# A four-layer graph megakernel: layer transitions in groups of five node blocks, narrower waits of tiles, node results in PSUM, and one edge list's bounds moved

## The chip, the cores and the metric

The kernel runs on one core of a Trainium2 chip. Its engines are PE (TensorE, matmul and transposes), DVE (VectorE), ACT (ScalarE), POOL (GpSimd, which here issues the indirect gathers and scatters) and SP (which issues the plain DMAs); each works through a queue of its own. The metric is the device time of one execution in microseconds, the median of several runs; lower is better.

## The reference

A node array x of 3125 rows by 256 floats goes through four pairs of layers. Each layer adds its result to x, and each sees the normalised rows of x.

```python
x = x + gat(norm(x), edges_A)                    # gnn0: 8 heads, relu
x = x + layernorm(z + top2_moe(z)), z = norm(x)  # ffn0: 16 experts, 2 per row
x = x + gat(norm(x), edges_A)                    # gnn1: 8 heads
x = x + layernorm(z + moe(z)), z = norm(x)       # ffn1: 2 of 8 experts for all rows
x = x + gat(gat(norm(x)))                        # gnn2: g2a (8 heads), g2b (1 head)
x = x + moe(z), z = norm(x)                      # ffn2: 4 experts, scores from attention over edges_B
x = x + edge_attention(norm(x), edge_attr)       # gnn3
x = x + moe(norm(x))                             # ffn3: 8 experts, two hidden layers, batch norm
```

`norm` subtracts a row's mean and divides by its standard deviation. `gat` is attention over a list of edges: a projection h of every node, a logit per edge from the source's and the target's h, a softmax over the edges that arrive at one node, and the weighted sum of the sources' h. List A has 50,000 edges, sorted by target; list B has 65,536 in random order.

## The kernel before

Nodes lie in 25 blocks of 128 (`NT` = 25, `NP` = 3200 with padding), one row per partition; `self.xs` holds x in SBUF for the whole run. Edges lie 128 partitions deep: A with 391 per partition, B with 512. A scheduler (the tile framework) sets the order on each engine, from the program's order and the dependences between tiles; only the inner loops over edges are put on DVE and ACT by hand (`manual_schedule`). Memory comes in pools. A tile of a pool takes over bytes that an earlier tile used, and waits until that one's users are done.

A graph layer (`gat_once`) goes like this. `norm` computes `bn_stats` and `bn_aggr` of all 25 blocks (`stats`), one square root on ACT and one reciprocal, then 25 times z. `transposed` turns each z block into zT by PE with a copy by ACT. A projection per block follows (`hps`): its values and source logits go to a DRAM table by SP, its target logits into `D`, copied by DVE. `spread` scatters D (25 indirect DMAs of POOL, the `A_Z` scatter) to the first edge of each node, reads that back, and spreads it along the edges. Then comes the loop over edges: POOL gathers the sources' rows (`hg`, one indirect DMA for 128 edges), DVE and ACT weigh and accumulate them, and SP writes groups of eight columns back to `OUT`. `join_chunks` repairs the nodes whose edges cross partitions. `node_results` then gathers each node's row from OUT (`ng`, 25 gathers, in groups of `NB` = 5 blocks), divides by the sum of the weights, and hands the group to `use`, which adds it to x or writes it to z. For g2a, g2b and ffn2 the node's own term is added (`own`, in a tile `nown`). Both work in place in `ng`, and `ng` has three buffers.

For each list the kernel needs bounds, the first and last edge of every node (`bounds`): a comparison of 128 by 3200 and its sum on DVE, an index, then 25 gathers of whole rows of targets by POOL (`brow`), each counted by one DVE operation (`bjunk`), and some twenty small ones. `marks` computes where runs of edges begin, and penalties (`penG`) for the scans. List B has to be sorted first; that runs on DVE beside gnn0's gathers (`sort_packed`), and B's bounds and marks are the end of the same function. They are first needed in ffn2.

The expert layers: ffn0 takes logits of all blocks (`token_logits`), top 2, and scatters rows to 40 slots of one expert each; at the end POOL gathers two results per row (`y`), and `add_layernorm` (L1044 to L1046 and the addition to x, L762) normalises and adds. ffn1 picks two experts for everybody from the mean of zT, and runs each over seven blocks of up to 512 rows. ffn2 deals its 28 units of expert work (4 experts by 7 blocks of rows) to the eight groups of 64 gathers of list B, six to each group until none is left; in each group the copy of a part of the edge features from DRAM to DRAM (`copy_features`) follows the group's units in the program, and SP issues it in that order. ffn3 runs softmax, loads batch-norm columns, adds the biases (`gb`), and then 8 experts by 7 blocks.

Of the kernel before, what the change touches and what calls it, by code (L numbers as in the profile page):

```python
# [9 lines left out]
F32 = mybir.dt.float32  # L10
# [4 lines left out]
ALU = mybir.AluOpType  # L15
AX = mybir.AxisListType
PSUM = bass.MemoryType.PSUM
DRAM = bass.MemoryType.DRAM

P = 128  # L20
# [13 lines left out]

class Edges:
# [3 lines left out]
class Kernel:  # L39
    def __init__(self, tc, ctx, a, out):  # L40
        self.tc, self.nc, self.a, self.out = tc, tc.nc, a, out
        nc = self.nc
        self.const = ctx.enter_context(tc.tile_pool(name="const", bufs=1))
        self.dram = ctx.enter_context(tc.tile_pool(name="dram", bufs=1, space=DRAM))
# [39 lines left out]
    def columns(self, pool, aps, rows_each, name):  # L84
# [5 lines left out]
        with tc.tile_pool(name=name + "_l", bufs=1) as lp, tc.tile_pool(name=name + "_p", bufs=1, space=PSUM) as pp:  # L90
# [9 lines left out]
    def stats(self, pool, src, nt, name):  # L100

        nc = self.nc
        mv = pool.tile([P, nt, 2], F32, name=name + "_mv")
        for t in range(nt):
            st = pool.tile([P, 6], F32, name=name + "_st", bufs=4)
            nc.vector.bn_stats(st, src[:, t, :])  # L106
            nc.vector.bn_aggr(mv[:, t, :], st)
        rs = pool.tile([P, nt], F32, name=name + "_rs")
        nc.scalar.activation(rs, mv[:, :, 1], AF.Sqrt, bias=self.eps5)  # L109
        nc.vector.reciprocal(rs, rs)  # L110
        return mv, rs

    def norm(self, pool, z):

        mv, rs = self.stats(pool, self.xs, NT, "ln")
        for t in range(NT):
            self.nc.vector.tensor_scalar(z[:, t, :], self.xs[:, t, :], mv[:, t, 0:1], rs[:, t : t + 1], op0=ALU.subtract, op1=ALU.mult)  # L117

    def transposed(self, psum, z, zT):

        nc = self.nc
        for t in range(NT):
# [3 lines left out]
            nc.scalar.copy(zT[:, :, t * P : (t + 1) * P], ps)  # L126

# [14 lines left out]
    def edges_by_destination(self, name, src_ap, dst_ap, E, zc):  # L142
# [10 lines left out]
        with tc.tile_pool(name="s0", bufs=1) as sp:  # L153
# [21 lines left out]
            with tc.tile_pool(name="sp0", bufs=1, space=PSUM) as pp:  # L175
# [25 lines left out]
    def counting_sort(self, L, src, dst, dstf):  # L201
# [4 lines left out]
        with tc.tile_pool(name="s1", bufs=1) as sp, tc.tile_pool(name="s2", bufs=2) as wp:  # L206
# [21 lines left out]
            with tc.tile_pool(name="sp1", bufs=1, space=PSUM) as pp:  # L228
# [21 lines left out]
            with tc.tile_pool(name="sp2", bufs=2, space=PSUM) as pp:  # L250
# [98 lines left out]
    def sort_packed(self, name, src_ap, dst_ap, E, zc):  # L349
# [7 lines left out]
        with ExitStack() as scope:  # L357
# [17 lines left out]
            table = self.dram.tile([P, T], F32, name=name + "_dst")  # L375
            nc.sync.dma_start(out=table, in_=dstf)
            self.bounds(L, sp, table, dstf)
            dnext = sp.tile([P, 1], F32, name="dnext")
            nc.vector.memset(dnext, -5.0)
            nc.sync.dma_start(out=dnext[: P - 1, :], in_=table[1:, 0:1])  # L380
            self.marks(L, sp, dstf, dnext)
        return L

    def bounds(self, L, sp, table, dstf):
# [4 lines left out]
        with tc.tile_pool(name="bw", bufs=3) as wp, tc.tile_pool(name="bp", bufs=1, space=PSUM) as pp:  # L389
# [78 lines left out]
    def chain_marks(self, L, sp, dstf):  # L468
# [14 lines left out]
        with tc.tile_pool(name="cmp", bufs=1, space=PSUM) as pp:  # L483
# [34 lines left out]
    def spread(self, L, D, z, n, tag):  # L518
# [6 lines left out]
        with tc.tile_pool(name=tag + "z", bufs=1) as sp:  # L525
# [12 lines left out]
    def att_weights(self, pool, load_w, a_src, a_dst, H, dh, tag):  # L538
# [5 lines left out]
        with tc.tile_pool(name=tag + "aw", bufs=2) as sp:  # L544
# [9 lines left out]
    def gat_once(self, L, tag, load_z, load_w, a_src, a_dst, H, dh, eps, loops, use):  # L554
# [11 lines left out]
        with tc.tile_pool(name=tag + "k", bufs=1) as kp:  # L566
# [9 lines left out]
            with tc.tile_pool(name=tag + "t", bufs=1) as sp, tc.tile_pool(name=tag + "tp", bufs=3, space=PSUM) as pp:  # L576
# [3 lines left out]
                self.transposed(pp, z, zT)  # L580
                for t in range(NT):
# [7 lines left out]

            R = kp.tile([P, W], F32, name="R")  # L590
            mR = kp.tile([P, H], F32, name="mR")
            with tc.tile_pool(name=tag + "e", bufs=1) as sp, tc.tile_pool(name=tag + "v", bufs=4) as vp, \
                    tc.tile_pool(name=tag + "vp", bufs=2, space=PSUM) as pp, \
# [79 lines left out]
    def node_results(self, L, tag, OUT, H, dh, eps, own, use):  # L673
# [6 lines left out]
        with tc.tile_pool(name=tag + "n", bufs=3) as np_:  # L680
            for t in range(0, NT, NB):
# [4 lines left out]
                r = np_.tile([P, NB, H], F32, name="nr")  # L686
                den = gv[:, :, :, dh]
                val = gv[:, :, :, :dh]
                wide = lambda x: x.unsqueeze(3).to_broadcast([P, NB, H, dh])
                if own is not None:  # L690

                    mx = np_.tile([P, NB, H], F32, name="nmx")
# [9 lines left out]
                    nc.vector.tensor_tensor(c, c, r.unsqueeze(1).to_broadcast([P, 2, NB, H]), ALU.mult)  # L702
                    ho = np_.tile([P, NB, Fh], F32, name="nown")
                    nc.vector.tensor_tensor(vals(ho), vals(own[1][:, t : t + NB, :W])[:, :, :, :dh], wide(c[:, 1]), ALU.mult)
                    nc.vector.tensor_tensor(val, val, wide(c[:, 0]), ALU.mult)
                    nc.vector.tensor_tensor(val, val, vals(ho), ALU.add)
                else:
                    nc.vector.tensor_scalar(r, den, eps, None, op0=ALU.add)
                    nc.vector.reciprocal(r, r)
                    nc.vector.tensor_tensor(val, val, wide(r), ALU.mult)  # L710
                use(t, NB, val, np_)

    def join_chunks(self, L, tag, OUT, R, mR, H, dh):
# [5 lines left out]
        with tc.tile_pool(name=tag + "j", bufs=1) as sp, tc.tile_pool(name=tag + "jp", bufs=1, space=PSUM) as pp:  # L719
# [44 lines left out]
    def normed(self, pool):  # L764
        z = pool.tile([P, NT, C], F32, name="z")
        self.norm(pool, z)
        return z
# [7 lines left out]
    def gnn0(self, L):  # L775
        nc, tc, a = self.nc, self.tc, self.a
        with tc.tile_pool(name="g0", bufs=1) as sp:
# [771 lines left out]
```

## Time and profile before

| | |
|---|---|
| time, median of 3 runs | 6270.55 us (6269.11 to 6270.8) |
| the profiled execution | 6277.97 us, its span 6275.9 us |
| granted TensorE clock, mean | 0.677 |
| busy | PE 41%, DVE 56%, ACT 13%, POOL 51% of the span |
| POOL `hg` of gnn0 and gnn1, 782 gathers | 969 ns each |
| POOL `hg` of ffn2, 512 gathers | 1014 ns each, 232.9 us idle before them |
| the edge loops: gnn0, gnn1, g2a, g2b, ffn2 | 152 to 655, 1440 to 1930, 2325 to 2814, 2941 to 3429, 3575 to 4327 us |
| the edge loop of gnn3 | 4556 to 5540 us |
| experts: ffn0, ffn1, ffn3 | 898 to 1272, 2066 to 2230, 5715 to 6275 us |

Times within the profile are microseconds from the start of the span, and durations are those of single instructions in it. A line names the engine, the source line, the operation and its tiles (output, arrow, inputs); in square brackets stands how long the engine had been idle, and what ended that. L129 is the helper that issues every gather, so gathers are told apart by their tiles. A row of the waits has the total in us, the number of times and the longest. PEclk is the granted clock of TensorE, in tenths of full speed. Between the stretches of the table lie the transitions from one layer to the next.

### The profile page before, as it was taken

What the parts mean: (1) busy time and instruction counts of PE and PEld (TensorE: products, weight loads), DVE (VectorE), ACT (ScalarE), POOL (GpSimd) and SP (SyncE); (2) the same over time, 40 slices, a digit from 0 to 9 for tenths busy, and PEclk for the clock granted to TensorE, in tenths of its full rate; (3) what the DMA queues carried; (4) which work ended last, traced back from release to release, by engine and by line L of the source; (5) the groups of instructions that cost most, each with busy time, mean ns of one, the idle gap of its engine ahead of it and who ended that gap; (6) DMA issues with size and microseconds to landing.
All of it is one profiled execution on the core that took longest, in us unless ns stands there. A gap on an engine that the chain in (4) does not pass through costs nothing. (4 is left out here: it accounts for less than half of the span.)

```text
span 6275.9 us, 39477 instructions
## 1 busy us (share of the span) xinstructions
PE 2584.4 (41%) x9265; PEld 1734.2 (28%) x9265; DVE 3504.1 (56%) x8011; ACT 794.9 (13%) x1810; POOL 3231.9 (51%) x3326
## 2 busy tenths in 40 slices
PE   2000049920001940002000499400566666639999
PEld 1000037710000530001000355200244555525555
DVE  6998611156886268884777411112778888871111
ACT  1000012210001110001000122100011111102222
POOL 3777430037774137775776576675077777730000
PEclk9555569955555975555555699755777666657999
DMA  5566335416663026663666234522377888730000
GB/s 193 191 225 221 124 115 169 156 57 197 223 219 109 14 64 224 220 218 109 212 212 204 52 109 123 154 55 67 144 256 262 264 268 262 264 123 16 10 11 26
DMA packets 398594, 963.74 MB, mean 154 GB/s; under 512 B 92478, under 2 KB 241053, under 8 KB 365966
## 3 DMA queue, kind: packets, MB, share of 16 engines
q1 hardware_dynamic: 236254, 538.71, 23.9%
q0 software_dynamic: 162096, 422.40, 23.2%
q8 instruction: 77, 1.26, 0.1%
q14 instruction: 167, 1.37, 0.1%
HBM read 611.38 MB, written 400.71 MB: 161 GB/s over the span
## 5 line engine op out<-in xcount | busy, mean ns | idle before, releaser
L724 PE MATMUL mRT<-ident,mR 128*8 128x128 f32 (+2 forms) x6 | 2.2, 372 | 2230.5 <-DVE mR L613 1356.0
L129 POOL DMA_INDIRECT hg<-g_H,A_tab x782 | 758.1, 969 | 240.4 <-issue 225.0
L668 DVE SCALAR_TENSOR_TENSOR hg<-hg,A_keep,v 128x264 f32<-128x264 f32 (+1 forms) x1368 | 666.2, 487 | 44.2
L129 POOL DMA_INDIRECT hg<-f_H,B_tab x512 | 519.3, 1014 | 232.9 <-issue 148.2
L724 PEld LDWEIGHTS mRT<-ident,mR 128*8 128x8 f32 (+2 forms) x6 | 0.5, 82 | 2233.1 <-issue 2233.1
L913 PE MATMUL ape<-we,aT 128*128 128x256 f32 x1564 | 493.6, 487 | 150.9 <-DVE kv L932 147.3
L129 POOL DMA_INDIRECT kv<-g_KV,A_tab x391 | 370.9, 949 | 295.3 <-issue 279.3
L660 DVE TENSOR_TENSOR v<-hg,e 128x1056 f32<-128x1056 f32 (+1 forms) x392 | 488.0, 1245 | 3.6 <-ACT e L652 3.6
L913 PEld LDWEIGHTS ape<-we,aT 128*128 128x128 f32 x1564 | 384.3, 252 | 251.1 <-DVE kv L932 164.4
L129 POOL DMA_INDIRECT hg<-g2a_H,A_tab x391 | 372.8, 953 | 119.2 <-issue 106.7
L129 POOL DMA_INDIRECT hg<-g2b_H,A_tab x391 | 371.5, 950 | 119.2 <-issue 114.0
L129 POOL DMA_INDIRECT q<-g_Q,A_tab x391 | 370.8, 948 | 120.1 <-issue 105.2
L1386 DVE TENSOR_TENSOR l<-hg,ad 128x256 f32<-128x256 f32 x8 | 6.3, 790 | 632.0 <-DMA hg<-f_H,B_tab 632.0
L1501 DVE SCALAR_TENSOR_TENSOR xs<-ps,g,xs 128x256 f32<-128x256 f32 x200 | 94.2, 484 | 458.1 <-PE ps L1500 458.1
L652 ACT ACTIVATE e<-d 128x72 f32<-128x72 f32 (+1 forms) x245 | 54.8, 223 | 2141.0 <-DVE d L649 2141.0
L125 PE MATMUL tr<-ident,z 128*128 128x128 f32 x450 | 109.5, 374 | 498.2 <-DVE z L117 434.6
L134 POOL DMA_INDIRECT A_Z<-D,A_first x100 | 99.3, 993 | 356.1 <-PE hps L584 223.4
L907 PE MATMUL apt<-ident,at 128*128 128x128 f32 x782 | 193.1, 382 | 196.6 <-ACT aT L909 188.2
L129 POOL DMA_INDIRECT y<-f_Y,pos x50 | 47.5, 949 | 398.3 <-DMA f_Y<-y 383.4
L125 PEld LDWEIGHTS tr<-ident,z 128*128 128x128 f32 x450 | 71.6, 200 | 535.1 <-ACT ln_rs L109 316.6
L1494 ACT ACTIVATE hT<-ps,bn 128x512 f32<-128x512 f32 (+1 forms) x224 | 162.4, 731 | 390.5 <-PE ps L1492 390.5
L930 DVE TENSOR_TENSOR kj<-kv,ape 128x512 f32<-128x512 f32 x196 | 135.9, 693 | 132.3 <-PE ape L913 112.1
(476 smaller groups left out, 6471.9 us busy)
## 6 DMA issues: line engine op xcount, KB each, us to landing
g_OUT<-hg SPq DMA_DIRECT2D x96, 1088.0 KB, 5.0
g2a_OUT<-hg SPq DMA_DIRECT2D x48, 1088.0 KB, 4.9
g_OUT<-kv SPq DMA_DIRECT2D x48, 1088.0 KB, 6.4
g2b_OUT<-hg SPq DMA_DIRECT2D x48, 1032.0 KB, 4.6
at<-attr SPq DMA_DIRECT2D x48, 1024.0 KB, 4.9
w<-in_L_ffn_w_dram SPq DMA_DIRECT2D x80, 512.0 KB, 3.9
attr<-in_edge_attr_dram SPq DMA_DIRECT2D x5, 6256.0 KB, 25.7
attr<-in_edge_attr_dram SPq DMA_DIRECT2D x3, 6240.0 KB, 26.9
```

Source lines behind the costliest of these rows:

```text
L125: nc.tensor.transpose(ps[:, k, :], z[:, t, k * P : (k + 1) * P], self.ident)
L129: return self.nc.gpsimd.indirect_dma_start(out=out, out_offset=None, in_=table, in_offset=bass.IndirectOffsetOnAxis(ap=idx, axis=0))
L134: i = self.nc.gpsimd.indirect_dma_start(out=table, out_offset=bass.IndirectOffsetOnAxis(ap=idx, axis=0), in_=in_, in_offset=None)
L652: nc.scalar.activation(e, d, AF.Exp)
L660: nc.vector.tensor_tensor(vals(v)[:, :k], vals(g[:, j0 : j0 + k, :W]), e[:, :, j0 + 1 : j0 + k + 1].rearrange("p h n -> p n h").unsqueeze( ...
L668: nc.vector.scalar_tensor_tensor(to, prev, L.keep[:, t + j0 + j : t + j0 + j + 1], v[:, j, :], op0=ALU.mult, op1=ALU.add)
L907: nc.tensor.transpose(pt[:, i2, k, :], at[t][:, j + i2, k * P : (k + 1) * P], self.ident)
L913: nc.tensor.matmul(pe[:, i2, :], aT[:, i2, k, :], we[:, k, :], start=(k == 0), stop=(k == KC - 1))
L930: nc.vector.tensor_tensor(kj[:, :k2], g[:, j : j + k2, :C], pe[:, :k2], ALU.add)
L1386: nc.vector.tensor_tensor(ln, g[:, :, W:].rearrange("p n h -> p h n"), ad[:, t : t + GB, :H].rearrange("p n h -> p h n"), ALU.add)
L1494: nc.scalar.activation(hT[:, f, :n], ps[:, :n], AF.Relu, bias=bn[l][1][:, c0 : c0 + 1], scale=bn[l][0][:, c0 : c0 + 1])
L1501: nc.vector.scalar_tensor_tensor(self.xs[:, t, :], po, g[:, t, e : e + 1], self.xs[:, t, :], op0=ALU.mult, op1=ALU.add)
```

## The change

It has seven parts.

1. All pools are opened with `reuse_waits="tile"`: a tile then waits for the users of the bytes that it takes over, and not for those of the whole pool before it.
2. `norm` and `add_layernorm` work in groups of five blocks: statistics, square root, reciprocal and z of one group, then the next.
3. `transposed` takes a function that is called after each block, so projections and logits follow each block's transposes in the program. `token_logits` adds its bias per group of five.
4. `node_results` puts the factors (`nf`) and the result (`nout`) into PSUM; `use` gets the result there. The tile `nown` is gone.
5. B's bounds and marks move out of `sort_packed` into `finish_sorted`, which is called after ffn1 and loads the sorted targets back from DRAM.
6. One tile z serves gnn0 to gnn2 with ffn0 and ffn1, instead of one for each layer.
7. ffn2's units of expert work are dealt by four to a group of gathers.

```diff
+def pool_of(tc, **kw):
+    return tc.tile_pool(reuse_waits="tile", **kw)
...
     def norm(self, pool, z):
-        mv, rs = self.stats(pool, self.xs, NT, "ln")
-        for t in range(NT):
-            self.nc.vector.tensor_scalar(z[:, t, :], self.xs[:, t, :], mv[:, t, 0:1], rs[:, t : t + 1], op0=ALU.subtract, op1=ALU.mult)
+        for t0 in range(0, NT, NB):
+            mv, rs = self.stats(pool, self.xs, t0, NB, "ln")
+            for t in range(NB):
+                self.nc.vector.tensor_scalar(
+                    z[:, t0 + t, :], self.xs[:, t0 + t, :], mv[:, t, 0:1], rs[:, t : t + 1], op0=ALU.subtract, op1=ALU.mult)
-    def transposed(self, psum, z, zT):
+    def transposed(self, psum, z, zT, then=None):
...
             nc.scalar.copy(zT[:, :, t * P : (t + 1) * P], ps)
+            if then is not None:
+                then(t)
...
-            self.bounds(L, sp, table, dstf)
-            dnext = sp.tile([P, 1], F32, name="dnext")
-            nc.vector.memset(dnext, -5.0)
-            nc.sync.dma_start(out=dnext[: P - 1, :], in_=table[1:, 0:1])
-            self.marks(L, sp, dstf, dnext)
         return L
+    def finish_sorted(self, L, sp):
+        nc = self.nc
+        dstf = sp.tile([P, L.T], F32, name="dstf3")
+        nc.sync.dma_start(out=dstf, in_=L.table)
+        self.bounds(L, sp, L.table, dstf)
+        dnext = sp.tile([P, 1], F32, name="dnext")
+        nc.vector.memset(dnext, -5.0)
+        nc.sync.dma_start(out=dnext[: P - 1, :], in_=L.table[1:, 0:1])
+        self.marks(L, sp, dstf, dnext)
...
-        with tc.tile_pool(name=tag + "n", bufs=3) as np_:
+        with pool_of(tc, name=tag + "n", bufs=3) as np_, pool_of(tc, name=tag + "np", bufs=1, space=PSUM) as pp:
...
+                out = pp.tile([P, NB, Fh], F32, name="nout")
...
-                    nc.vector.tensor_tensor(c, c, r.unsqueeze(1).to_broadcast([P, 2, NB, H]), ALU.mult)
-                    ho = np_.tile([P, NB, Fh], F32, name="nown")
-                    nc.vector.tensor_tensor(vals(ho), vals(own[1][:, t : t + NB, :W])[:, :, :, :dh], wide(c[:, 1]), ALU.mult)
-                    nc.vector.tensor_tensor(val, val, wide(c[:, 0]), ALU.mult)
-                    nc.vector.tensor_tensor(val, val, vals(ho), ALU.add)
+                    f = pp.tile([P, 2, NB, H], F32, name="nf", bufs=2)
+                    nc.vector.tensor_tensor(f, c, r.unsqueeze(1).to_broadcast([P, 2, NB, H]), ALU.mult)
+                    nc.vector.tensor_tensor(vals(out), vals(own[1][:, t : t + NB, :W])[:, :, :, :dh], wide(f[:, 1]), ALU.mult)
+                    nc.vector.tensor_tensor(val, val, wide(f[:, 0]), ALU.mult)
+                    nc.vector.tensor_tensor(vals(out), val, vals(out), ALU.add)
                 else:
-                    nc.vector.tensor_scalar(r, den, eps, None, op0=ALU.add)
-                    nc.vector.reciprocal(r, r)
-                    nc.vector.tensor_tensor(val, val, wide(r), ALU.mult)
-                use(t, NB, val, np_)
+                    f = pp.tile([P, NB, H], F32, name="nf", bufs=2)
+                    nc.vector.tensor_scalar(f, den, eps, None, op0=ALU.add)
+                    nc.vector.reciprocal(f, f)
+                    nc.vector.tensor_tensor(vals(out), val, wide(f), ALU.mult)
+                use(t, NB, vals(out), np_)
...
-        mv, rs = self.stats(pool, y, NT, "ln2")
-        for t in range(NT):
+        for t0 in range(0, NT, NB):
+            mv, rs = self.stats(pool, y, t0, NB, "ln2")
+            for t in range(t0, t0 + NB):
...
-                    for u in units[i * 6 : i * 6 + 6]:
+                    for u in units[i * 4 : i * 4 + 4]:
                         expert(*u)
...
-    with tc.tile_pool(name="s4", bufs=1) as k.sort_pool, tc.tile_pool(name="sortp", bufs=1, space=PSUM) as k.sort_psum:
-        k.gnn0(A)
-        B = k.sort_packed("B", a["L2_ffn_edge_index"][0], a["L2_ffn_edge_index"][1], 65536, 8)
-    k.ffn0()
-    k.gnn1(A)
-    k.ffn1()
-    k.gnn2(A)
+    with pool_of(tc, name="z", bufs=1) as zp:
+        k.z = zp.tile([P, NT, C], F32, name="z")
+        with pool_of(tc, name="s4", bufs=1) as k.sort_pool, pool_of(tc, name="sortp", bufs=1, space=PSUM) as k.sort_psum:
+            k.gnn0(A)
+            B = k.sort_packed("B", a["L2_ffn_edge_index"][0], a["L2_ffn_edge_index"][1], 65536, 8)
+        k.ffn0()
+        k.gnn1(A)
+        with pool_of(tc, name="s5", bufs=1) as sp:
+            k.ffn1()
+            k.finish_sorted(B, sp)
+        k.gnn2(A)
     k.ffn2(B)
```

## Prediction

> **What bounds the kernel now.** I read the page's 40 slices first, to see whether one engine carries the whole span.
>
> ```profile
> PE   2000049920001940002000499400566666639999
> DVE  6998611156886268884777411112778888871111
> POOL 3777430037774137775776576675077777730000
> PEclk9555569955555975555555699755777666657999
> ```
>
> None does. POOL issues gathers in the attention layers, PE runs the expert blocks, and between them lie transitions in which no engine is full and TensorE is granted half its clock. The change touches the transitions, so I cut the timeline there and asked, with the busy times by stretch and the waits of each stretch, what ends last. The first is gnn0 to ffn0:
>
> ```profile
> 722.00:767.00 45.00, 1.76 (x6) 1.12 (x6) 23.90 (x76) 0.00 (x0) 24.15 (x26) 0.50 0.45 147
> 767.00:830.00 63.00, 33.83 (x157) 31.29 (x158) 34.83 (x179) 12.42 (x29) 0.08 (x1) 0.53 0.02 5
> ```
> ```profile
> L129 POOL DMA_INDIRECT brow<-B_dst,at x25: 943/947/1601, 721.6 to 757.5; - x25
> L412 DVE SCALAR_TENSOR_TENSOR bjunk<-brow,node,ones x25: 750/752/777, 725.5 to 761.0; 128x512 f32<-128x512 f32 x25
> ```
> ```profile
> DVE bjunk L412 <- DMA brow<-B_dst,at: 19.5, 25, 2.3
> PE tr L125 <- DVE z L117: 13.6, 1, 13.6
> ```
>
> Columns of the stretches: length; busy PE, weight loads, DVE, ACT, POOL; clock; DMA. In the first 45 us nothing runs but list B's bounds, 25 gathers each answered by one DVE count. Only then come the norm's statistics, and PE waits for the first z until 779.2. The second place is ffn1 to gnn2a:
>
> ```profile
> 2230.03 0.48 DVE L1035 SCALAR_TENSOR_TENSOR z<-ps,f_pr,z 128x256 f32<-128x256 f32 x1 [2.35 <-PE ps L1034]
> ...
> 2269.31 0.40 DVE L106 BATCH_NORM_STATS2 ln_st<-xs 128x6 f32<-128x256 f32 x1
> ```
>
> Between these lines lies all of add_layernorm: 100 DVE operations at 0.335 us spacing after PE has finished. The third is node_results, in the timeline of g2a:
>
> ```profile
> 2846.12 0.95 POOL L129 DMA_INDIRECT ng<-g2a_OUT,A_end  x1 [0.30 <-issue]
> ...
> 2846.78 1.49 DVE L704 TENSOR_TENSOR nown<-hs_all,nc 128x1280 f32<-128x1280 f32 x1
> 2847.37 1.72 POOL L129 DMA_INDIRECT ng<-g2a_OUT,A_end  x1 [0.30 <-issue]
> ```
>
> A gather takes 0.95 us alone and 1.1 to 2.3 beside a wide DVE operation with both inputs in SBUF. Over that 0.95 the 25 gathers lose 3.8, 4.1, 4.8, 4.9, 0 and 3.7 us in gnn0, gnn1, g2a, g2b, f2 and gnn3. Beside L660 and L668, which have an operand in PSUM, the excess is under 0.01 us a gather.
>
> **The change part by part.** Starts and waits come from the profiled execution (span 6275.9, 6278.0 with what lies around it, 7.4 above the median); the order within each engine comes from the built program.
>
> *Bounds leave gnn0 (-50).* B's marks and bounds no longer stand between gnn0's last x (722.4) and ffn0's statistics. The first z needs some ten statistics (3.9 us at 0.39) and the 2.1 us that the square root and its table took before: 728.5. PE starts at 729 instead of 779.2. The 25 tiles of transposes and logits stay PE's (1.17 us each at half clock), and top2, routing and experts follow: -50.
>
> *Bounds arrive behind ffn1 (+20).* add_layernorm in groups runs between expert 1's tiles, DVE being idle for about 8 us before each block of four. After the last tile (2230.5, statistics to 2230.9) DVE does the comparison (3.5), the reduction (3.5), the last group's 17 operations that stand before the index copy (5.7) and small ones: index at 2244.5. POOL's 25 gathers and counts take the 40.1 us that they took in gnn0: 2284.6. Behind them on DVE stand the rest of the bounds (3.4), the weights' attention columns (2.7; their load is issued only at the next to last count, and is hidden by the rest), 0.5 of memsets, 25 statistics (9.8), 20 z (6.7) and roots; then the first D, 2308, and POOL's A_Z scatter at 2309 instead of 2289.2. SP's reload of the destinations is queued in gnn1's tail, and PE's transpose behind the last expert tile costs 0.3. B's penalties and marks, some 4 us of DVE, fall into gnn1's waits for gathers.
>
> *Square roots between GELUs (0).* [...] Each of four groups adds two table loads to ACT's queue in expert 1. The trace has a load at 1.28 us with the next activation 0.01 behind it. [...] ACT idles 8.0 us before each block's GELUs. In the worst group, which ends with a block's fourth tile, the first GELU comes 1.0 us late by the trace [...]; PE has three PSUM buffers of 1.7 us ahead. By the row 0[...]. I take 0.
>
> *Other norms.* Statistics and z become groups, but DVE's order still puts the D copies behind all statistics and 20 of 25 z, so a layer whose scatter waits for D gains only 5 z and the root: -2.5 in gnn1, -3 in f2. ffn0's add_layernorm leaves 90 of 100 operations behind the y gathers: 0. In gnn0 z now stands behind the bounds, not between their counts (+8); PE and POOL then find D ready and lose the 2 us steps of the first copies: -2, between +5 and -4. Where PE is the bound it starts with the first group: ffn1 -5, gnn3 -7 (first z at 4451 instead of 4458.2, then 92 us of PE), ffn3 -3.7. ffn3's batch-norm columns and first weights still wait for the last transposes and gb.
>
> *g2b (-6).* The projection's weights were loaded after the last z (2891.8) and hps started at 2900.5. Their bytes now come free with g2a's results, so their DMA runs before, and the first D comes at about 2897 instead of 2903.9.
>
> *Node results in PSUM (-27).* The stretched gathers go: -2.5 in gnn0 (L784 keeps two SBUF inputs), -4 in gnn1, -3.7 in gnn3, nothing in f2. In g2a and g2b POOL also waited 3.8 and 9.0 us for an ng tile that the use still read; it now comes free one or two 1.49 us operations earlier. What is late next is DVE: -6 in g2a, -5 in g2b. That makes -21; with g2b's -6 above it is the -27. [...]
>
> ```profile
> L1035 DVE SCALAR_TENSOR_TENSOR z<-ps,f_pr,z x50: 482/484/484, 2066.3 to 2230.0; 128x256 f32<-128x256 f32 x50
> ...
> L1202 DVE SCALAR_TENSOR_TENSOR z<-y,f_pr,z x50: 477/484/486, 1280.4 to 1341.2; 128x256 f32<-128x256 f32 x50
> ```
>
> Same 484 ns from PSUM and SBUF. [...] by the row nothing. A write of DVE to PSUM isn't in the trace; I take the SBUF price.
>
> *f2's experts, 6 to 4 units (+10).* A unit is 17.05 us of PE, so 68 us fit under the gathers' 92. But SP issues the feature copy behind the units' outputs, and gathers stall for it:
>
> ```profile
> 4052.51 0.56 SPq L960 DMA_DIRECT2D attr<-in_edge_attr_dram  x1
> ...
> 4064.40 0.95 POOL L129 DMA_INDIRECT hg<-f_H,B_tab  x1 [2.18 <-DMA hg<-f_H,B_tab]
> 4070.73 0.95 POOL L129 DMA_INDIRECT hg<-f_H,B_tab  x1 [5.38 <-DMA hg<-f_H,B_tab]
> ```
>
> A copy by itself costs 10.7 to 12.4 us; the four that fell together with DVE's own 7 us of disturbance cost 6 to 8.5. With four units the copies come inside the groups, by themselves: up to +17, and -10 if they miss the gathers. I take +10.
>
> Sum: -50 +20 -2.5 -3 -2 -5 -7 -3.7 -27 +10 = -70. From 6278.0 that is 6208 in a profile, and 6270.5 - 70 = 6200 as the median.
>
> **The rivals.**
> (1) Contention stays, since a gather collides with any wide DVE operation, or writes to PSUM are slow: L660 and L668 speak against it. Without the 21 us the time is 6221.
> (2) The second transition pays the whole bounds, because the table loads or 24 additions of add_layernorm stop PE: some 30 us more, 6230. Against: the 8 us gaps of DVE and ACT.
> (3) Narrower waits let more start early (copies, y loads, z between statistics) and f2 loses nothing: -35 more, 6165. For: g2b's weights show the pattern; against: I found only that one load on a path.
> (4) Slower: f2's experts are now bursts with pauses of some 24 us. If the granted clock doesn't come back in a burst, ACT's exponent, queued behind the group's units, holds the gathers. The gain of 70 is lost when a group takes 10 us more than its 92, four units at 0.67 of the clock; at 0.5 they take 136 us, 7 x 44 = 308 more: 6500. Against: right after 0.50 in ffn3's transition, the first 85 us of experts show 0.97.
> (5) The change doesn't shorten what it groups: for gnn1 and f2 I already count that; if ffn0 gained nothing, the time would be 6250.
>
> **How the numbers follow.** Forecast 0.64, with a range of its own of 6172 to 6228; (1) 0.10; (2) 0.08; (3) 0.12; (4) 0.04; (5) with other losses, near no change, 0.02. A measurement of this kernel tells 0.2% (12.5 us) from nothing. Low 6155, high 6240: outside lie (4), (5) and the tails of (2) and (3).
>
> **What would show it.** Right: first tr of ffn0 near 725; from ffn1's last expert tile to g2a's first scatter about 79 us instead of 58.7, with the bjunk counts in it; ng gathers all near 0.95; eight copies with 10 to 12 us of DMA stalls each in f2. Wrong: PE gaps in ffn1's expert 1, nout operations above 1.5 us, f2's units over 17 us, or a loop of hg that isn't the old length.

## The result and the profile after

The changed kernel takes 6226.9 us in the median of four runs (6222.8 to 6228.5), the kernel before 6270.1 beside it: a ratio of 0.993, with a 95% interval from 0.9913 to 0.9947. That is 43 us faster. A repetition on another chip gave 6225.7 against 6269.2, ratio 0.9931 (0.9917 to 0.9944). The forecast was 6200, with a range from 6155 to 6240: the sign and the size are right, but 27 of the 70 us did not come. The profiled executions lie further apart than the medians (span 6275.9 before, 6223.5 after, 52.4 us): the one before was some 8 us above its median, the one after 1.6 below its own. So about 9 of the missing 27 us are the choice of the profiled execution, and about 18 are terms of the sum. The page of the changed kernel, 40 slices:

```profile
PE   2000259820002920002000756740656666649999
...
DVE  6998611168885468875776410112678888862111
...
POOL 3777330047773057766776566764077777730000
PEclk9555579965555965556555778875876666657999
```

It still has the shape of before: no engine is full throughout, and PE's clock is near half in the slices of transitions. The stages are what to compare. The first transition, from gnn0's last x at 722.1, in busy times by stretch (length; PE, weight loads, DVE, ACT, POOL; clock; DMA):

```profile
722.00:727.00 5.00, 0.09 (x1) 0.09 (x2) 5.00 (x26) 0.60 (x2) 0.00 (x0) 0.50 0.00 0
727.00:765.00 38.00, 34.02 (x150) 29.32 (x150) 17.05 (x92) 11.19 (x29) 0.00 (x0) 0.50 0.00 1
```

The 45 us in which only the bounds ran are gone, PE has its first z at 726.5 instead of 778.6, and works through 38 us at clock 0.50. Before it needed 30.2 us for the same 25 blocks of transposes and logits. Where the bounds went is seen in the group of their gathers (ns min/median/max, first and last start) and in the timeline from ffn1's last expert tile to g2a's first scatter:

```profile
L138 POOL DMA_INDIRECT brow<-B_dst,at x25: 944/945/947, 2186.7 to 2222.0; - x25
```

```profile
2172.07 0.48 DVE L1056 SCALAR_TENSOR_TENSOR z<-ps,f_pr,z 128x256 f32<-128x256 f32 x1 [2.35 <-PE ps L1055]
...
2172.94 3.47 DVE L408 TENSOR_TENSOR cmp<-heads,node 128x3200 f32<-128x3200 f32 x1
...
2186.72 0.94 POOL L138 DMA_INDIRECT brow<-B_dst,at  x1 [177.62 <-DVE z L1068]
...
2226.28 0.42 DVE L111 BATCH_NORM_STATS2 ln_st<-xs 128x6 f32<-128x256 f32 x1
...
2251.14 1.01 POOL L143 DMA_INDIRECT A_Z<-D,A_first  x1 [28.24 <-DVE D L602]
```

The last expert tile is added at 2172.07. Add_layernorm's last group follows at once, the comparison (3.47) and the index are ready for POOL at 2186.7, the 25 gathers and counts last to 2226.2, and then come the statistics of g2a and its first scatter at 2251.14: 79.1 us, where the kernel before took 59.2 from the same point. The third place is g2a's node results:

```profile
2825.01 0.95 POOL L138 DMA_INDIRECT ng<-g2a_OUT,A_end  x1 [2.54 <-DVE nmx L712]
...
2826.26 0.95 POOL L138 DMA_INDIRECT ng<-g2a_OUT,A_end  x1 [0.30 <-issue]
2826.30 1.50 DVE L723 TENSOR_TENSOR nout<-hs_all,nf 128x1280 f32<-128x1280 f32 x1
2827.51 0.94 POOL L138 DMA_INDIRECT ng<-g2a_OUT,A_end  x1 [0.30 <-issue]
2827.70 1.48 DVE L724 TENSOR_TENSOR ng<-ng,nf 128x1280 f32<-128x1280 f32 x1
```

```profile
L730 DVE TENSOR_TENSOR nout<-ng,nf x15: 1477/1486/1497, 685.3 to 5573.6; 128x1280 f32<-128x1280 f32 x15
...
L801 DVE TENSOR_TENSOR y<-nout,bias x5: 1471/1475/1491, 686.9 to 719.1; 128x1280 f32<-128x1280 f32 x5
```

Where a gather took 1.1 to 2.3 us beside a wide operation of DVE, it now takes 0.94 or 0.95 beside L723, which has its output and its factors in PSUM, and also beside L724, which has only its factors there (a wait of 2.54 for DVE is left). DVE's own time hardly changes: the median of L730 is 1486 ns, and that of the same product in the kernel before (L710), with all its tiles in SBUF, 1478; that of L801, which reads the result, is 1475, and 1481 before (L782).

By stage, the lead over the kernel before (in brackets the step since the line above, and what the sum had for it):

| reached | before | after | lead |
|---|---|---|---|
| gnn0's last x | 722.4 | 722.1 | 0.3 (0.3; 4.5) |
| gnn1's first scatter | 1403.8 | 1353.2 | 50.6 (50.3; 52.5) |
| gnn1's last x | 1994.4 | 1940.8 | 53.6 (3.0; 4) |
| ffn1's last expert tile | 2230.0 | 2172.1 | 58.0 (4.4; 5) |
| g2a's first scatter | 2289.2 | 2251.1 | 38.1 (-19.9; -20) |
| g2a's last z | 2891.7 | 2847.4 | 44.3 (6.2; 6) |
| g2b's first scatter | 2904.8 | 2854.1 | 50.7 (6.4; 6) |
| g2b's last x | 3517.6 | 3458.4 | 59.2 (8.5; 5) |
| f2's first scatter | 3540.3 | 3480.6 | 59.7 (0.5; 3) |
| f2's last gather of edges | 4326.9 | 4277.5 | 49.4 (-10.3; -10) |
| gnn3's last projection | 4551.0 | 4498.3 | 52.7 (3.3; 7) |
| gnn3's last x | 5631.6 | 5576.9 | 54.7 (2.0; 3.7) |
| ffn3's last logit | 5670.8 | 5618.5 | 52.3 (-2.4; 3.7) |

A second trace of the changed kernel (e9) has each step behind the first line within a microsecond of these; of the kernel before there is one trace. (What g2a works out goes to z, so its row ends with the last z.) The large terms came as summed. What is missing is spread over gnn0 (4.2), gnn3's projections (3.7) and ffn3 (6.1), and smaller pieces.

### The profile page after: what moved, and what is told of

It reads as the page before. It is cut to its first block, busy times and chain, and to the rows that moved or that the text cites. A ratio compares the mean times of both kernels' runs of the same rounds, so it can differ in the third digit from the quotient of the medians.

```text
span 6223.5 us, 39484 instructions
## 1 busy us (share of the span) xinstructions
PE 2625.8 (42%) x9265; PEld 1748.1 (28%) x9265; DVE 3505.2 (56%) x8059; ACT 817.7 (13%) x1862; POOL 3205.3 (52%) x3326
## 5 line engine op out<-in xcount | busy, mean ns | idle before, releaser
L1389 PE MATMUL ps<-zT,w 128*128 128x512 f32 (+1 forms) x448 | 194.0, 584 | 199.8 <-ACT hT L1390 199.8
L928 PE MATMUL apt<-ident,at 128*128 128x128 f32 x782 | 192.3, 380 | 198.0 <-ACT aT L930 191.2
```

The costliest lines, as they stand in the source:

```text
L928: nc.tensor.transpose(pt[:, i2, k, :], at[t][:, j + i2, k * P : (k + 1) * P], self.ident)
L1389: nc.tensor.matmul(ps[:, :n], w1[:, k, f * P : (f + 1) * P], zT[:, k, b0 : b0 + n], start=(k == 0), stop=(k == KC - 1))
```

## The experiments

Theories at the start: T1, a loop PE to ACT to DVE to PE stretches the transitions that PE bounds; T2, the order of PE's queue (a projection right behind its block) does. Beside them stand the forecast's own terms, each to be undone by itself; only part 6 of the change, the one tile z, was not undone. Runs e1 to e4 shared a chip (before: 6273.1), e9 to e11 another (6269.2), e12 a third (6275.7). Runs e5 to e8 fell on a chip on which the kernel before takes 7182.3 us: loops of gathers are slower there (gnn0's 563 to 573 us instead of 507; e7, which does not differ from the changed kernel up to there, has L1305 of ffn1 at 2159.5 us instead of 1978.7), while ffn0's transposes and logits, where nothing is gathered, take 37.8 us there as in the changed kernel. So for those four I read stages, and totals only as ratios.

**e1 and e2: what stretches the transposes.** The timeline of the changed kernel in ffn0 shows the loop of T1:

```profile
735.54 0.80 ACT L133 COPY zT<-tr 128x256 f32<-128x256 f32 x2 [0.35 <-PE tr L132]
736.24 0.30 ACT L114 ACTIVATE ln_rs<-ln_mv,eps 128x5 f32<-128x5 f32 x1
736.57 0.19 DVE L115 RECIPROCAL ln_rs<-ln_rs 128x5 f32<-128x5 f32 x1 [4.13 <-ACT ln_rs L114]
...
736.80 1.70 DVE L123 TENSOR_SCALAR z<-xs,ln_mv,ln_rs 128x256 f32<-128x256 f32 x5
...
737.36 2.96 PE L132 MATMUL tr<-ident,z 128*128 128x128 f32 x10 [1.42 <-DVE z L123]
```

A group's square root (L114) stands in ACT's queue behind the copies of transposed blocks (L133) of the group before. DVE has its statistics but waits 4.13 us for the root, z comes late, and PE stands idle for 1.42 us. e1 takes the groups out of `norm`:

```diff
-        for t0 in range(0, NT, NB):
-            mv, rs = self.stats(pool, self.xs, t0, NB, "ln")
+        for t0 in range(0, NT, NT):
+            mv, rs = self.stats(pool, self.xs, t0, NT, "ln")
```

> The norm in one group of 25 blocks again, the projection of a block still behind its transposes. T1 (what stretched PE's transposes after the change is the loop PE to ACT to DVE: a later group's square root stands in ACT's queue behind the copies of earlier blocks, so the next z comes late): the stretches of ffn0, ffn3 and gnn3 (37.8, 38.2 and 98.2 us from the first transpose to the last projection) go back to about 31, 31 and 92, but the first z comes later by the 20 statistics that it need not wait for now (7.8 us at 0.39); the two cancel, total within 6 us of the changed kernel's 6227. T2 (the order of PE's queue, the projection behind each block, makes PE wait for ACT's copies): the stretches stay at 37 to 39 and the three starts come 7.8 us later: 6227 + 23 = 6250.

e2 keeps the groups and takes the projections out of the loop over blocks:

```diff
             nc.scalar.copy(zT[:, :, t * P : (t + 1) * P], ps)
-            if then is not None:
-                then(t)
+        if then is not None:
+            for t in range(NT):
+                then(t)
```

> The norm in five groups, but projections and logits in a loop of their own behind all transposes, as before the change. T1 (square root behind the copies in ACT's queue): the z of a later group is as late as now, the stretches of ffn0 and ffn3 stay at about 38 us, total 6227 within 6. T2 (order of PE's queue): the stretches go back to 30.3 (ffn0), 30.3 (ffn3) and 92 (gnn3), with the early start kept: 6227 - 21 = 6206.

Measured: e1 6246.2 us, ratio 0.9954 (0.9940 to 0.9967); e2 6226.9, ratio 0.9924 (0.9910 to 0.9937). From the first transpose to the last projection:

| | before | after | e1 | e2 |
|---|---|---|---|---|
| ffn0 | 30.2 | 37.8 | 33.5 | 38.0 |
| ffn3 | 30.3 | 38.2 | 33.4 | 38.3 |
| gnn3 | 92.2 | 98.1 | 99.5 | 92.7 |

The waits in ffn0, of the changed kernel, then of e2, then of e1 (in us: total, times, longest; the longest is each time the wait for the first z):

```profile
PE tr L132 <- DVE z L123: 60.1, 3, 57.0
...
DVE ln_rs L115 <- ACT ln_rs L114: 6.2, 3, 4.1
```

```profile
PE tr L132 <- DVE z L123: 60.3, 3, 57.0
```

```profile
PE tr L132 <- DVE z L123: 63.5, 1, 63.5
```

Neither theory holds alone. In ffn0 and ffn3 T1 explains the larger part: without the groups the gaps for z are gone (one wait is left, that for the first) and 4.3 and 4.8 us come back, of 7.6 and 7.9. The other 3.3 us of ffn0 are no waiting, for PE is idle for only 0.3 us of e1's stretch. They fit the order of PE's queue as it was built. In the kernel before, transposes and logit products alternate, first below; in e1, second, they stand in long runs of one kind:

```profile
793.96 0.87 PE L1058 MATMUL lps<-gw,zT 128*128 128x16 f32 x4
794.68 0.67 PE L125 MATMUL tr<-ident,z 128*128 128x128 f32 x2
795.14 0.87 PE L1058 MATMUL lps<-gw,zT 128*128 128x16 f32 x4
```

```profile
742.99 7.58 PE L132 MATMUL tr<-ident,z 128*128 128x128 f32 x26
750.36 4.29 PE L1082 MATMUL lps<-gw,zT 128*128 128x16 f32 x20
754.49 1.09 PE L132 MATMUL tr<-ident,z 128*128 128x128 f32 x4
```

From start to start a transpose takes 0.23 us and a logit product 0.18 where they alternate, and 0.28 and 0.21 in these runs; over the 26 transposes and four runs of 20 products that makes some 3.6 us. The order that e2 got has such runs too (20 and 18 products), so e2 did not bring back the order of the kernel before, and that it changes nothing here does not speak against T2. Groups with an alternating order were not run. In gnn3 T2 is right: there a block has 3.7 us of projections, z is never late, and e2 alone brings the time back. Its loss is in the wait for the copy of the block just transposed, here in the changed kernel; e2 has no such wait for qps:

```profile
PEld qps L889 <- ACT zT L133: 4.1, 8, 0.7
...
PE qps L889 <- ACT zT L133: 1.9, 7, 0.5
```

The waits explain about half of gnn3's 5.4 us; the rest I could not place. Both edits together were not run. In all e1 comes near T2's 6250: the first z is 6.4 to 7.6 us later in ffn0, gnn3 and ffn3, ffn0 and ffn3 get 4 to 5 of it back, and gnn3 nothing.

**e3: six units per group in f2.**

```diff
-                    for u in units[i * 4 : i * 4 + 4]:
+                    for u in units[i * 6 : i * 6 + 6]:
```

> Six expert units per group of gathers in f2 instead of four, all else as changed. If the feature copies that fall by themselves are what the gathers lose (my forecast: +10 for four units, 11.7 found), the loop of hg in f2 goes from 763.6 us back to about 752 and the total to 6227 - 12 = 6215. Rival: the loop is longer for another reason (waits by tile, experts started earlier, ACT's order): the loop stays near 763 and the total within 4 us of 6227.

Measured: 6219.5 us, ratio 0.9913 (0.9900 to 0.9927), 7 us under e2 beside it; the loop of gathers takes 754.8 us, instead of 763.6 in the changed kernel and 768.7 to 772.3 in e1, e2 and e4, which have four units on the same chip. POOL's waits for a gather to land, in the changed kernel and in e3:

```profile
POOL hg L138 <- DMA hg<-f_H,B_tab: 97.9, 30, 5.5
```

```profile
POOL hg L138 <- DMA hg<-f_H,B_tab: 89.6, 29, 5.6
```

This is the forecast's step as written. In both kernels SP issues eight copies of features. In the changed kernel each falls by itself into a group, and the gathers wait 10 to 14 us behind it. With six units the first four fall together with DVE's own disturbance, and the waits behind each of these come to 8 or 9 us; behind the last four they stay at 13 to 14.

**e4: node results in SBUF.**

```diff
-                out = pp.tile([P, NB, Fh], F32, name="nout")
+                out = np_.tile([P, NB, Fh], F32, name="nout", bufs=1)
```

and the factors `nf` likewise; the PSUM pool falls away.

> Node results and their factors in SBUF tiles of their own instead of PSUM, the order of operations as changed. [...]the excess of the ng gathers over 0.95 us comes back (some 4 us in gnn0, gnn1, g2a, g2b, gnn3) and the waits for ng in g2a and g2b partly too: 6227 + 15 = 6242, ng phases of g2a and g2b at 37 to 42 us instead of 33 to 34. Rival: the gain came from the shorter use of the ng tile (results no longer written back into it, waits by tile), not from the memory: ng phases stay at 33 to 35 and the total within 5 us of 6227.

Measured: 6251.8 us, ratio 0.9966 (0.9952 to 0.9979): 25 us above e2 beside it, which is as fast as the changed kernel. The timeline of g2a's node results in e4:

```profile
2834.28 2.30 POOL L138 DMA_INDIRECT ng<-g2a_OUT,A_end  x1 [0.30 <-issue]
2834.34 1.43 DVE L723 TENSOR_TENSOR nout<-hs_all,nf 128x1280 f32<-128x1280 f32 x1
...
2837.23 1.48 DVE L725 TENSOR_TENSOR nout<-ng,nout 128x1280 f32<-128x1280 f32 x1
2838.63 1.48 DVE L724 TENSOR_TENSOR ng<-ng,nf 128x1280 f32<-128x1280 f32 x1
2838.99 1.95 POOL L138 DMA_INDIRECT ng<-g2a_OUT,A_end  x1 [1.01 <-DVE nout L725]
```

A gather beside L723, now with inputs and output in SBUF, takes 2.30 us; one beside L724 takes 1.95, after a wait of 1.01 for L725. From the last gather of edges (in gnn3 from the first gather of results) to the last x, e4 needs 3.0, 5.6, 3.4, 6.2 and 4.0 us more than the changed kernel in gnn0, gnn1, g2a, g2b and gnn3: 22.3 together. The memory is the cause, and not the shorter use of the gathered tile.

**e5 and e12: the bounds and the groups of add_layernorm.** e5 puts the bounds back behind gnn0:

```diff
             B = k.sort_packed("B", ...)
+            with pool_of(tc, name="s5", bufs=1) as sp:
+                k.finish_sorted(B, sp)
...
-        with pool_of(tc, name="s5", bufs=1) as sp:
-            k.ffn1()
-            k.finish_sorted(B, sp)
+        k.ffn1()
```

> List B's bounds and marks back behind gnn0, all else as changed: the move undone by itself. By my sum the move was worth -50 in the first transition and +20 in the second, -30 in all: 6227 + 30 = 6257, with the first z of ffn0 some 48 us later than now and the way from ffn1's last expert tile to g2a's first scatter at about 55 to 59 us instead of 79. Rival: the first transition was shortened by the groups (its norm starts with five blocks), and the move brings less than 20: total below 6247.

Measured: ratio 0.9876 (0.9858 to 0.9894), no different from e6 on the same chip (0.988), which has the bounds behind ffn1 (and the wider waits). The first z of ffn0 comes 60.0 us after gnn0's last x, 55.7 later than in e6, so the groups do not shorten this transition. But at the other end, from ffn1's last expert tile:

```profile
2405.38 0.48 DVE L1056 SCALAR_TENSOR_TENSOR z<-ps,f_pr,z 128x256 f32<-128x256 f32 x1 [2.35 <-PE ps L1055]
...
2416.43 0.42 DVE L782 TENSOR_TENSOR xs<-xs,z 128x256 f32<-128x256 f32 x1
...
2434.49 1.01 POOL L143 DMA_INDIRECT A_Z<-D,A_first  x1 [193.02 <-DVE D L602]
```

29.1 us to g2a's scatter, not 55 to 59. The move by itself therefore gives 52 to 56 us in one place (by the first z, against the kernel before and against e5) and takes 50 to 53 in the other (against the changed kernel and e6): it is worth about nothing. What shortened the second transition is something else in the change, and of what lies there only add_layernorm's groups come into question: in e5 its last addition ends 11 us after the last tile, in the kernel before 38. e12 tests this at the fourth corner:

```diff
-        for t0 in range(0, NT, NB):
-            mv, rs = self.stats(pool, y, t0, NB, "ln2")
-            for t in range(t0, t0 + NB):
+        for t0 in range(0, NT, NT):
+            mv, rs = self.stats(pool, y, t0, NT, "ln2")
+            for t in range(t0, t0 + NT):
```

> add_layernorm in one group of 25 again, B's bounds behind ffn1 as changed: the fourth corner beside the kernel before (bounds in gnn0, one group: 58.7 us from ffn1's last expert tile to g2a's first scatter), the run with the bounds back in gnn0 (five groups: 29.2) and the changed kernel (bounds behind ffn1, five groups: 79.1). If the +20 of my sum is in truth +50 for the bounds and -29.5 for add_layernorm's groups, and both add up, since DVE's order puts all 100 operations of add_layernorm ahead of the counts: 79.1 + 25 to 29 = 104 to 108 us, total 6226 + 27 = 6253. Rival: the 100 operations fill DVE's time between the counts (about 21 of the bounds' 40 us are free), the way is 85 to 92 us and the total 6232 to 6239.

Measured: 6257.9 us, ratio 0.9973 (0.9963 to 0.9983), and in the timeline:

```profile
2172.20 0.48 DVE L1056 SCALAR_TENSOR_TENSOR z<-ps,f_pr,z 128x256 f32<-128x256 f32 x1 [2.35 <-PE ps L1055]
...
2278.64 1.01 POOL L143 DMA_INDIRECT A_Z<-D,A_first  x1 [27.95 <-DVE D L602]
```

106.4 us. The four corners, last expert tile to scatter:

| | add_layernorm in one | in five groups |
|---|---|---|
| bounds in gnn0 | 59.2 (before) | 29.1 (e5) |
| bounds behind ffn1 | 106.4 (e12) | 79.1 (after) |

Both effects add up: the bounds cost 47 to 50 here, the groups save 27 to 30.

**e6: waits by pool.**

```diff
-    return tc.tile_pool(reuse_waits="tile", **kw)
+    return tc.tile_pool(**kw)
```

> Tiles wait for the users of the whole released pool again, as before the change, all else as changed. By my sum the narrower waits matter at one place, the projection weights of g2b (-6), where the way from g2a's last x to g2b's first D was 12.2 us before and is 6.3 now: 6227 + 6 = 6233, and that way back at 11 to 12. Rival (my third case of the forecast): they matter in more places, 20 to 35 us: 6247 to 6262.

Measured: ratio 0.988 (0.986 to 0.9901). From g2a's last z to g2b's first D 7.0 us (after 6.3, before 12.2); last expert tile to scatter 82.1 (after 79.1); from the last x to the first z of ffn0 and ffn3, to ffn1's first expert tile and to f2's first scatter, within 1.2 us of the changed kernel. The load of g2b's projection weights, in the changed kernel and in e6:

```profile
L778 SPq DMA_DIRECT2D g2b_w<-in_L_gnn_W_dram x1: 379/379/379, 2834.2 to 2834.2; - x1
```

```profile
L778 SPq DMA_DIRECT2D g2b_w<-in_L_gnn_W_dram x1: 379/379/379, 3115.4 to 3115.4; - x1
```

With narrow waits it starts 13 us ahead of the last z (2847.4), with pool waits still 1.5 ahead of it (3116.9), in the kernel before 0.1 behind it. So the narrow waits are worth about 1 us here and at most some 3 in the second transition, where the two traces come from different chips.

**e7 and e10: hiding the bounds.** e7 calls `finish_sorted` inside ffn1, ahead of the expert blocks:

```diff
+            before_experts()
             self.experts(2, F, load1, load2, ...
...
-            k.ffn1()
-            k.finish_sorted(B, sp)
+            k.ffn1(lambda: k.finish_sorted(B, sp))
```

> finish_sorted is called inside ffn1, before its expert blocks, where POOL is idle for 163 us; all else as changed. If what the second transition pays is only POOL's 25 gathers with their counts standing alone (40 us with DVE's comparison and reduction ahead of them), they go beside the experts, and the way from ffn1's last expert tile to g2a's first scatter falls from 79 to about 40 us: 6227 - 39 = 6188. Rival: DVE's 30 us of bounds come between the tiles that PE waits for (evictions of the expert blocks), and PE's expert phase grows by as much as the end saves: total within 8 us of 6227, expert phase 192 us now, 210 or more then.

Measured: ratio 0.9845 (0.9827 to 0.9863). The way behind the last tile falls to 30.6 us, but the expert phase grows from 193 to 234: from gnn1's last x to g2a's scatter it is 304.8 us, in e6 313.3. Only 8.5 us are left of the gain, so the rival is nearly right, though by another mechanism than it named. PE's and POOL's timeline:

```profile
2217.68 0.67 PE L439 MATMUL pnext<-both,nxt 128*128 128x50 f32 x2 [55.51 <-DVE both L431]
...
2221.20 9.10 PE L1049 MATMUL ps<-zT,w 128*128 128x512 f32 x16 [0.33 <-DVE B_end L462]
```

```profile
2213.07 0.94 POOL L138 DMA_INDIRECT brow<-B_dst,at  x1 [0.61 <-DVE bjunk L427]
2217.41 0.95 POOL L138 DMA_INDIRECT w<-in_L_ffn_W_dram,idx  x1 [3.40 <-DVE chunk L430]
```

PE's product with the bounds stands in its queue ahead of the experts and waits 55.5 us, and the experts' weights stand in POOL's queue behind the bounds' 25 gathers. e10 cuts `bounds` in two at that product:

```diff
     def finish_sorted(self, L, sp):
-        self.bounds(L, sp, L.table, dstf)
+        yield from self.bounds(L, sp, L.table, dstf)
...
+        yield
         nc.vector.scalar_tensor_tensor(chunk, lb[:, :NT], float(T), chunk, ...
...
     def experts(..., beside):
                 load2(e, w2)
+                if e == E - 1:
+                    next(beside)
...
             self.experts(2, F, load1, load2, ..., beside)
+            for _ in beside:
+                pass
```

> B's bounds are cut in two: the rows that each node block needs, with their 25 gathers and counts, are issued with the last expert's weights and may run wherever POOL and DVE are free in ffn1, and the part with TensorE's two products comes behind the experts. What it tests: that the bounds themselves cost the second transition about 50 us (79 with them, 29 in the run with the bounds back in gnn0), and that the run with the bounds ahead of the experts lost this again because the experts' weight gathers stood behind the bounds' 25 in POOL's queue and PE's queue held the product with the bounds. Then the way from ffn1's last expert tile to g2a's scatter is 29 to 33, up to 20 of the 25 counts (0.75 us each) lie on the router's chain, and the time is 6227 - 50 + 15 = 6192. Rival: the 29 came from somewhere else (groups of add_layernorm alone can't do it while the bounds are near); then the way stays above 50 and the total within 15 of 6227.

Measured: 6211.7 us, ratio 0.9907 (0.9892 to 0.9922), beside 6225.7 of the changed kernel. The way behind the last tile:

```profile
2201.58 0.48 DVE L1063 SCALAR_TENSOR_TENSOR z<-ps,f_pr,z 128x256 f32<-128x256 f32 x1 [2.35 <-PE ps L1062]
...
2234.05 1.01 POOL L143 DMA_INDIRECT A_Z<-D,A_first  x1 [197.04 <-DVE D L607]
```

32.5 us, as expected; but only 14 to 18 us of the 46 remain. In the built order 14 of the gathers stand in the router's chain, and the rest of the gain is lost in three places: node results of gnn1 start 5.6 us later, behind the comparison and the sum; the router takes 8.6 more; the experts' phase 13.7 more, of which PE's timeline shows two waits (the changed kernel's first weights came after 16.81):

```profile
2018.37 9.09 PE L1056 MATMUL ps<-zT,w 128*128 128x512 f32 x16 [21.57 <-DMA w<-in_L_ffn_W_dram,idx]
...
2039.29 3.72 PE L1062 MATMUL ps<-w,hT 128*128 128x256 f32 x8 [6.65 <-DVE z L1063]
```

**e8: two groups in `norm`.** Blocks 0 to 4, then 5 to 24, and projections in their own loop as in e2:

```diff
-        for t0 in range(0, NT, NB):
-            mv, rs = self.stats(pool, self.xs, t0, NB, "ln")
-            for t in range(NB):
+        for t0, n in ((0, NB), (NB, NT - NB)):
+            mv, rs = self.stats(pool, self.xs, t0, n, "ln%d" % n)
+            for t in range(n):
```

> The norm in two groups, of 5 and of 20 blocks, and projections in a loop of their own behind the transposes. After the two runs before: in ffn0 and ffn3 a later group's square root waits in ACT's queue behind copies of earlier blocks (about 3.3 us of PE waiting for z, in two gaps), in gnn3 the projection behind each block costs 5.5. With one later root there is one gap: PE's five first blocks take 5.9 us, the 20 statistics behind the first five z take 7.8 and the root 2, so about 4 us of waiting, partly filled by logits. ffn0 and ffn3 at 35 to 37 us instead of 38, gnn3 at 92 instead of 98: 6227 - 10 = 6217. Rival: the gap of the one large group is as long as the two small ones together and only gnn3 gains: 6221.

Measured: ratio 0.9804 (0.9785 to 0.9823), the best of its chip. Stretches: ffn0 34.5, ffn3 34.7 us. The wait for z in ffn0 after the first five blocks, once instead of twice and 1.7 us instead of 3.1:

```profile
PE tr L132 <- DVE z L123: 1.7, 1, 1.7
```

Gnn3's last projection comes 93.9 us behind its first z, 99.8 in e6, and from gnn1's last x to g2a's scatter it needs 305.8 us, 313.3 in e6 (up to some 4 of these are e6's wider waits). From g2b's last x to f2's first scatter it takes 13.4 us, in the changed kernel 22.2. So it gains more than the 10 us expected; the total can't be read from a ratio on that chip.

**e9 and e11: the changed kernel again, and the parts together.** e11 is e10 with the edits of e8 and e3.

> The changed kernel once more, as the measure for the two beside it on the same chip, since the four runs before fell on a chip where the kernel before takes 7182 us. No theory differs here: ratio 0.993 to the kernel before where that takes about 6270; where gathers are as slow as on that chip, 0.985 to 0.99.

> The same with the norm in two groups (5 and 20 blocks), projections in a loop of their own behind the transposes, and six expert units in f2. The parts as found one by one: -35 for the bounds, -7 in ffn0 and ffn3 with -6 in gnn3 and -6 in ffn1 and the attention layers, -10 for six units: about -64 from the changed kernel, 6163. If the parts overlap (DVE's counts meet the longer second group of statistics in ffn1): 6185.

Measured: e9 6225.7 us; e11 6170.9 (6163.6 to 6173.1), ratio 0.9838 (0.9825 to 0.9852). It beats both kernels, by 98 and 55 us, between the two numbers expected. From gnn1's last x to g2a's scatter it needs 280.4 us (e10 286.0, after 310.3), f2's gathers 748.6.

## Why the prediction was right or wrong

*Bounds leave gnn0 (-50).* Right in sum (50.3 to gnn1's scatter, with gnn1's norm), but one step of it failed: that the 25 tiles of transposes and logits stay PE's at 1.17 us each. The first transpose came at 726.9, two us earlier than forecast, and the stretch grew from 30.2 to 37.8. The 1.17 us a tile are 0.46 for two transposes and 0.71 for four products in the alternating order of the kernel before; the changed kernel has long runs of one kind, and 3.7 us of idle PE, most of it for a late z. A lead of 52.3 us at the first transpose was 44.7 at the last logit. Up to gnn1's scatter it grew again to 50.6, by 2.9 us ahead of the rows' first scatter (829.9 and 782.3), where one addition of all logits became one per group, and by the rest up to gnn1's first D.

*Bounds arrive behind ffn1 (+20).* Right, step by step: index 14 us after the last tile, 39.5 us of gathers and counts (40.1 forecast), 25 more to the scatter. But the 20 is a difference, and e5 and e12 show what of: about +50 for the bounds and -30 for add_layernorm's groups. The forecast never wrote down the second number, so that it credited the move with 30 us that the groups had earned. My rival 2 (30 us more there) had no ground: expert phase 193.5 us before, 192.3 after.

*Square roots between GELUs (0).* Right: that expert phase, no longer than before, holds ten table loads where it held two. Each takes 1.28 us, and where its activation stood ready, that one starts 0.01 us behind it (a load at 2115.23, its GELU at 2116.52), as in the row of the forecast.

*Other norms.* ffn0's add_layernorm 0 is right, gnn1 and ffn1 nearly. Gnn3 (-7) and ffn3 (-3.7) are the wrong terms: 3.3 and +2.4. The step that failed is "where PE is the bound it starts with the first group" with PE's work held constant. It starts with it: the first z gains 5.5 us in ffn3 and 9.1 in gnn3. But the stretch that follows grows by 7.9 in ffn3, of which e1 gives back 4.8 (the square roots behind ACT's copies), and by 5.9 in gnn3, of which e2 gives back 5.4 (the order of PE's queue). I costed the groups from DVE's queue and left out ACT's and PE's.

*g2b (-6).* The number is right (6.4), the mechanism is not: e6 gives the narrow waits about 1 of it. In e4, with results in SBUF, the first D comes 2.8 us later than in the changed kernel, and in e2, with the projections behind all transposes, 0.9 later. The rest isn't settled.

*Node results in PSUM (-21).* -17 came between the kernels, and e4 loses 22.3. The SBUF price that the forecast took for DVE's reads and writes of PSUM held nearly: of the operations of 128 by 1280 that read or write `nout` or `nf`, L723 takes 1490 ns in g2a's mean, where the kernel before took 1463 (L704), and no other line rises by more than 10 ns in the mean of a layer. What fell short is the end of the phase: in gnn0 the gathers end 3.4 us earlier and x is done only 0.3 earlier, since DVE's order now leaves seven wide operations behind the last gather's landing instead of five. "What is late next is DVE" was written for g2a and g2b, where it did less harm (-5.5 and -8.8 for -6 and -5), and left out for the others.

*f2's experts (+10).* Right in size (10.3) and by its mechanism (e3); in e11 against e10, on one chip, six units shorten the loop by 16.6 us.

## What to carry to other kernels

A step that works in groups puts one small operation per group into every queue it touches (here a square root of 0.30 us, for which DVE waited 4.13 us behind ACT's copies): cost it in the queue of each engine, above all one that copies for the engine you want to start early. The price of a tile that is read from a trace holds for the order in which its parts stood there (a transpose 0.23 us and a logit product 0.18 where they alternated, 0.28 and 0.21 in long runs), so look at the order that the engine got. A term that is a difference of two changes in one place should be written as two terms, for only then is it seen which of them earns the time. And a block of work that is to be hidden brings all its queues along: what waits in it must stand behind the work that hides it, on each engine (in e7 one product of the bounds, ahead of the experts, held PE for 55.5 us).

## What I had not expected of the hardware

One chip ran the kernel before in 7182 us where the others took 6269 to 6276; gnn0's loop of gathers was longer there (563 to 573 us in e5 to e8 instead of 507), ffn0's transposes and logits were not (37.8 us). And a DVE operation of 128 by 1280 elements with its output and its factors in PSUM, one input still in SBUF, left the gathers beside it at 0.94 or 0.95 us, against 1.1 to 2.3 with everything in SBUF, at nearly the same time for itself (L723 1.47 to 1.50 us, L704 before 1.43 to 1.49). L724 does so with its factors alone in PSUM, at 0.94 or 0.95, so one input there is enough in this trace; whether the output alone would do was not tried.
